# Logits of a row tile in one visit, and one PSUM bank for each block product of the walk

## The chip, the cores and the metric

The kernel runs on one NeuronCore of a Trainium2 chip. Its measure is the device time in microseconds (us), median of several runs. A profile of one more execution gives a record of every instruction. Engines in it: PE is TensorE's matmuls, PEld its weight loads, DVE VectorE, ACT ScalarE, POOL GpSimd, SP the engine that issues most DMAs. Lines (L1109) are lines of the kernel before, unless it is said that they are the changed kernel's.

## The reference

Two layers on 2708 nodes with 256 features, each with a residual and a layer norm. Layer 0 takes two steps. In each, a bilinear attention over all nodes keeps, in every row, the largest probabilities up to a sum of 0.9 (top-p); beside it, the features walk over the adjacency matrix R with its rows normalised:

```python
q = X @ W1.T @ W2.T;  k = X @ W3.T;  logits = q @ k.T          # 64 wide
A = softmax(logits), cut per row to the top 0.9, renormalised   # top-p
R = adj + I;  R = R / R.sum(-1)
for n in range(2):                                              # steps
    A = top_p_attention(Xa); Xf = R @ Xf; Xa = A @ Xa
    Z = Z + Xf @ U1[n].T + Xa @ U2[n].T
x = layernorm(x + layernorm(X + Z))
```

Layer 1 is a graph attention with four heads of 64, masked by the adjacency matrix, with a softmax over the first axis; `x = layernorm(x + that)`. Everything is in 32-bit floats.

## The kernel before

**Row tiles.** The nodes are cut into 22 row tiles (`NT`), 16 of 128 rows and 6 of 110. For each row tile and step the kernel makes the logits against all nodes, the exponentials `e` (a row of 2708), the top-p search, and then the attention product.

**Attention.** `step` (L1307) goes over the row tiles, and `weigh` (L274) over six groups of column tiles (four tiles in each, two in the last): `turned` (L261) transposes a group of `e` on PE into the one transpose bank (`tr`), ScalarE copies it (`eT`), and PE multiplies. The transposes of the next group stand before the products of this one. After each group `between` calls `slot` (L1292), so a row tile has six slots, 0 to 5; the first transposes of the next row tile stand between slot 4 and slot 5.

**Slots.** A slot first advances the searches under way (`going`), then begins a new one for the row tile three ahead (in slot 4), advances the other work (`doing`: projections, norms, `sources` for layer 1) and the preparation of adjacency blocks (`mixes`, in step 0), and then spends a number of matmuls on the walk (`stream`, from `walks`, L1034), one matmul for each call. In step 1 the numbers are `SPEND_1`, 68 in a row tile. Engines keep the order in which the code writes this down (a manual schedule): every engine is a queue in that order, and waits come from data and buffers.

**Logits and search.** `scores` (L780) makes the logits in three pieces, of 512, 512 and 330 columns in each half of the nodes. The two halves lie on 64 rows of PE each, and run beside each other into the two banks of an `lg` tile (`ps_lg`, two tiles, four banks). After two pieces it yields, so that the third piece follows in slot 5. In step 1 a search then takes twelve slots: `survey` makes four tallies on ScalarE, `bound` and `candidates`, `settle` (sorting, ties) and the masked row at L965 are VectorE's. L965 of one row tile is issued in slot 4, right before the first transposes that read it.

**The walk.** R @ Xf is done in blocks of two row tiles by a scheme of seven products (`PRODUCTS`) in place of eight, with 11 matmuls in each product; 11 row pairs and two steps make 154 products. Their operands are loaded three products ahead. Products are added up in four chains: X (1 and 2), Y (6 and 7), Z (5 and 3), W (4). A chain's second product goes on adding in the first one's bank. There are two banks for the walk (`walk0`, `walk1`), with the attention's bank as a third while it is free. When a product ends, ScalarE copies it (1, 2, 5) or VectorE adds it to an earlier one (6, 7, 4, 3: L1119 to L1129), and GpSimd makes one sum (L1135). When the walk of step 0 ends, `reblend` (L1173) remakes the operands for step 1. After the last products of step 1, `finish` (L1261) scales a row tile's walk on ScalarE (L1265), adds up, and hands over to `norms` and `sources`.

**PSUM.** Eight banks: four for logits, two for the walk, one for the attention, one for transposes. Small products (projections, `sources`) take a bank from `free_bank` (L650): a walk bank as long as the walk has not begun, an `lg` tile afterwards.

**Layer 1** (L1496) begins when layer 0's buffers are given back; its first VectorE row is `pt` at L1606.

Of the kernel before, what the change touches and what calls it, by code (L numbers as in the profile page):

```python
# [16 lines left out]
P = 128  # L17
# [19 lines left out]
SPEND_BETWEEN, SPEND_1 = 14, (12, 11, 11, 12, 11, 11)  # L37
# [8 lines left out]
def kernel(  # L46
# [505 lines left out]
    def fast_layer0(ep, adjp):  # L552
# [89 lines left out]
        p1, y1, y2 = (spare_u[:, k * HALF : (k + 1) * HALF] for k in range(3))  # L642
        u_rows = u_sb[:, 1].rearrange("p c s d -> p (c s) d")
        lines = [u_rows[:, k, :] for k in range(4)]
        lines += [spare_u[:, c : c + D] for c in (3 * HALF, 3 * HALF + D)]
# [134 lines left out]
        def scores(s, t):  # L780

            m = rows[t]
            cols = slice(off[t], off[t + 1])
            e = ep.tile([P, N], F32, name="e")
            halves = e.rearrange("p (h n) -> p h n", h=2)
            zp = small.tile([P, 3], F32, name="zp")
            for n, (c0, w) in enumerate(pieces):
                lg = ps_lg.tile([P, 2, CHUNK], F32, name="lg")
                for h in range(2):
                    part = slice(h * DA, (h + 1) * DA)  # L790
                    nc.tensor.matmul(  # L791
                        lg[:m, h, :w], qT[part, cols], kT[s][part, c0 : c0 + w],
                        start=True, stop=True,
                    )
                nc.scalar.activation(  # L795
                    halves[:m, :, c0 : c0 + w], lg[:m, :, :w], AF.Exp,
                    accum_out=zp[:m, n : n + 1],
                )
                if n == 1:
                    yield  # L800
            z = facts[s][0][:m, t : t + 1]
            nc.gpsimd.tensor_add(z, zp[:m, 0:1], zp[:m, 1:2])
            nc.gpsimd.tensor_add(z, z, zp[:m, 2:3])
            tau = new("tau", m)
            nc.gpsimd.tensor_scalar(tau, z, TOP_P, None, op0=ALU.mult)
            return e, z, tau

        def new(name, m):
            return small.tile([P, 1], F32, name=name)[:m]
# [191 lines left out]
        def blend(name, j0, j1, k):  # L1001
# [23 lines left out]
            1: ("D11", "B11", "X"), 2: ("A12", "B21", "X"), 6: ("S2", "T2", "Y"),  # L1025
            7: ("S3", "T3", "Y"), 5: ("S1", "T1", "Z"), 3: ("S4", "B22", "Z"), 4: ("D22", "T4", "W"),
# [7 lines left out]
        def walks():  # L1034
# [43 lines left out]
            last_bank = 1  # L1078
            for at, (s, i, n) in enumerate(queue):
                a, b = 2 * i, 2 * i + 1  # L1080
                m = rows[a]
                _, name, chain = PRODUCTS[n]
# [7 lines left out]
                if at % 7 == 0:  # L1090
                    use, over = {}, set()
                    xa, xb = (rowp.tile([P, D + 1], F32, name="xw", bufs=4) for _ in range(2))
                    if order_of(s, i) is THREE:
                        home = dict(zip("XYZW", ((7 * i + k) % 3 for k in (0, 1, 2, 6))))
                    else:
                        k = 1 if last_bank == 0 else 0
                        home = dict(X=k, Y=1 - k, Z=k, W=1 - k)
# [8 lines left out]
                last_bank = home[chain]  # L1106
                for j in range(PAIRS):
                    k = rows[2 * j]
                    nc.tensor.matmul(  # L1109
                        ac, blk[:k, j, :], MOVING[name](j, k, w),  # L1110
                        start=start and j == 0, stop=j == PAIRS - 1, skip_group_check=True,
                    )
                    if j == PAIRS - 1:
                        over.add(n)
                        left = ac[:, :HALF]
                        if n == 1:
                            nc.scalar.copy(p1[:m], left)
                        elif n == 6:
                            nc.vector.tensor_add(y1[:m], left, p1[:m])  # L1119
                        elif n == 7:  # L1120
                            nc.vector.tensor_add(y2[:m], left, p1[:m])
                        elif n == 2:
                            nc.scalar.copy(xa[:m, :w], ac)  # L1123
                        elif n == 5:
                            nc.scalar.copy(xb[:m, HALF : HALF + w], ac)
                        elif n == 4:
                            nc.vector.tensor_add(xb[:m, :HALF], left, y2[:m])
                        else:
                            nc.vector.tensor_add(xa[:m, HALF:D], left, y1[:m])  # L1129
# [4 lines left out]
                        if n in (5, 7) and {5, 7} <= over:  # L1134
                            nc.gpsimd.tensor_add(xb[:m, HALF:D], xb[:m, HALF:D], y2[:m])  # L1135
# [145 lines left out]
        going, doing, stored, owing = [], [], set(), set()  # L1281
        early, walked, blending, begun, rows_kept = [], [], [], [], []
# [24 lines left out]
        def step(s, cur, spend):  # L1307
            turned_first = None
            for t in range(NT):
# [11 lines left out]
                def between(n):  # L1321
# [18 lines left out]
                    slot(spend[n], (s, t + 3) if n == len(groups) - 2 else None)  # L1340
# [55 lines left out]
        with tc.manual_schedule(engines=engines):  # L1396
# [434 lines left out]
```

## Time and profile before

| | us |
|---|---|
| median of 3 runs (1533.94 to 1536.61) | 1533.94 |
| profiled execution | 1534.79 |
| its span, first to last instruction | 1532.7 |
| step 0, first transposes to the last attention rows, about | 72 to 443 |
| step 1, the same, about | 514 to 1189 |
| layer 1, from the first VectorE row to the end | 1184 to 1533 |

Busy times are unions of an engine's rows over the span. A busy PE is not PE at its peak: matmuls are pipelined and their ends are modelled, so distances from start to start are the better measure of what a row costs. A 32-bit matmul stands in the records as two rows, a transpose as one; a few records are missing. The granted clock was 0.995 of full speed over the span.

### The profile page before, as it was taken

The numbers are of one execution on the slowest core, as the hardware profiler recorded it, in microseconds if no ns is written. First come the engines' busy times: TensorE is split into PE (matmuls) and PEld (weight loads), VectorE is DVE, ScalarE is ACT, GpSimd is POOL, SyncE is SP. The second block draws the span as 40 slices with busy tenths as digits, with TensorE's granted clock in tenths as the row PEclk, the third lists the DMA queues.
The fourth block names the chain that finished last, engine by engine and source line by source line (L and its number), as shares of the span: only waits on it lengthen the run. The fifth ranks groups of instructions, "written<-read, shape, count | busy, mean of one in ns | idle before, by whom it ended". The sixth has DMA issues, their size and how long they took to land. (4 is left out here: it accounts for less than half of the span.)

```text
span 1532.7 us, 29967 instructions
## 1 busy us (share of the span) xinstructions
PE 1492.8 (97%) x10537; PEld 1064.6 (69%) x10537; DVE 1277.1 (83%) x3749; ACT 804.9 (53%) x1495; POOL 594.5 (39%) x959
## 2 busy tenths in 40 slices
PE   8999999999999999999999999999999999999996
PEld 4477777776778889988988888887898223433343
DVE  3699888999714978888889898989895998999996
ACT  3444444444326556655655666666653344456474
POOL 0046657566013323323454554544444310035143
PEclk9999999999999999999999999999999999999998
DMA  6288888878037755554564555555455355334331
GB/s 166 66 246 277 247 247 281 266 234 255 12 102 235 211 165 167 161 162 137 159 199 142 165 183 170 182 166 178 137 151 178 109 172 167 100 104 135 88 105 53
DMA packets 214488, 255.97 MB, mean 167 GB/s; under 512 B 42145, under 2 KB 180541, under 8 KB 214329
## 3 DMA queue, kind: packets, MB, share of 16 engines
q1 hardware_dynamic: 205622, 246.62, 53.7%
q10 hardware_dynamic: 8707, 7.35, 1.5%
q8 instruction: 85, 1.39, 0.4%
q14 instruction: 74, 0.61, 0.1%
HBM read 190.10 MB, written 62.44 MB: 165 GB/s over the span
## 5 line engine op out<-in xcount | busy, mean ns | idle before, releaser
L816 ACT ACTIVATE junk<-e,minus,rth 128x2708 bf16<-128x2708 f32 (+1 forms) x88 | 232.9, 2646 | 52.5 <-POOL rth L848 51.7
L271 ACT COPY eT<-tr 128x512 f32<-128x512 f32 (+5 forms) x264 | 141.5, 536 | 199.0 <-PE tr L266 196.5
L284 PE MATMUL att<-xm,eT 128*128 128x256 f32 (+3 forms) x968 | 230.8, 379 | 0.3 <-ACT xa L1325 0.3
L284 PE MATMUL att<-ba,eT 128*128 128x256 f32 (+3 forms) x968 | 230.9, 379 | 0.0
L1618 PE MATMUL acc<-pt,v 128*32 128x512 f32 (+3 forms) x2112 | 222.9, 543 | 2.1 <-DVE pt L1606 1.1
L1606 DVE SCALAR_TENSOR_TENSOR pt<-e,tj,blk 128x1024 f32<-128x1024 f32 (+3 forms) x176 | 186.6, 1125 | 8.3 <-ACT xw L1265 5.4
L284 PEld LDWEIGHTS att<-xm,eT 128*128 128x128 f32 (+3 forms) x968 | 169.6, 186 | 22.0 <-ACT xa L1325 0.7
L284 PEld LDWEIGHTS att<-ba,eT 128*128 128x128 f32 (+3 forms) x968 | 169.5, 186 | 22.0 <-ACT eT L271 0.8
L795 ACT ACTIVATE e<-lg 128x1024 f32<-128x1024 f32 (+1 forms) x132 | 121.0, 921 | 105.7 <-PE lg L791 102.2
L1109 PE MATMUL walk<-xe,blk 128*128 128x128 f32 (+3 forms) x1386 | 172.9, 275 | 1.2 <-ACT xw L1123 0.7
L1109 PEld LDWEIGHTS walk<-xe,blk 128*128 128x128 f32 (+1 forms) x1386 | 164.4, 187 | 11.4 <-issue 7.4
L1618 PEld LDWEIGHTS acc<-pt,v 128*32 128x32 f32 (+1 forms) x2112 | 73.4, 109 | 130.8 <-issue 76.2
L266 PE MATMUL tr<-ident,e 128*128 128x128 f32 (+3 forms) x968 | 147.5, 271 | 4.8 <-ACT eT L271 4.8
L266 PEld LDWEIGHTS tr<-ident,e 128*128 128x128 f32 (+3 forms) x968 | 111.3, 139 | 47.1 <-issue 26.7
L1109 PE MATMUL walk<-xm,blk 128*128 128x128 f32 (+3 forms) x1034 | 131.3, 277 | 5.4 <-DVE u_sb L1119 2.9
L1109 PEld LDWEIGHTS walk<-xm,blk 128*128 128x128 f32 (+3 forms) x1034 | 124.2, 188 | 14.0 <-issue 6.1
L1628 PE MATMUL acc<-pt,sb 128*32 128x512 f32 (+3 forms) x1056 | 115.7, 542 | 0.0
L1606 DVE SCALAR_TENSOR_TENSOR pt<-r,tj,blk 128x1024 f32<-128x1024 f32 (+1 forms) x88 | 109.9, 1312 | 1.3 <-issue 0.6
L247 ACT ACTIVATE blk<-blk 128x1024 f32<-128x1024 f32 (+3 forms) x66 | 63.3, 960 | 82.5 <-DMA blk<-in_adjT_dram 76.2
L896 DVE MAX8 cand<-e 128x8 f32<-128x170 f32 (+1 forms) x352 | 85.9, 320 | 21.1 <-ACT e L795 21.0
L896 DVE MAX8 cand<-scr 128x8 f32<-128x97 f32 (+1 forms) x616 | 102.8, 244 | 0.0
L914 DVE MAX8 top<-work 128x8 f32<-128x128 f32 (+3 forms) x242 | 82.3, 340 | 8.3
(283 smaller groups left out, 2410.2 us busy)
## 6 DMA issues: line engine op xcount, KB each, us to landing
blk<-in_adjT_dram SPq DMA_DIRECT2D x68, 512.0 KB
blk<-S SPq DMA_DIRECT2D x48, 512.0 KB
blk<-D SPq DMA_DIRECT2D x24, 512.0 KB
blk<-in_adjT_dram SPq DMA_DIRECT2D x26, 440.0 KB
D<-blk SPq DMA_DIRECT2D x16, 512.0 KB
S<-scr SPq DMA_DIRECT2D x16, 512.0 KB
S<-blk SPq DMA_DIRECT2D x16, 512.0 KB
xm<-S SPq DMA_DIRECT2D x16, 512.0 KB
```

Source lines behind the costliest of these rows:

```text
L247: nc.scalar.activation(bar, bar, AF.Sign)
L266: nc.tensor.transpose(tr[: rows[t], q, :m], e[:m, off[t] : off[t + 1]], ident[:m, :m])
L271: copy(eT[:k, : len(grp), :m], tr[:k, : len(grp), :m])
L284: nc.tensor.matmul(acc, eT[: rows[t], q, :m], value(t), start=(t == 0), stop=(t == NT - 1),)
L795: nc.scalar.activation(halves[:m, :, c0 : c0 + w], lg[:m, :, :w], AF.Exp, accum_out=zp[:m, n : n + 1],)
L816: nc.scalar.activation(junk[:m], e[:m], func, scale=rth, bias=minus1[:m], accum_out=acc)
L896: nc.vector.max(cand[:, n, :], src[:m, n * size : min(N, (n + 1) * size)])
L914: nc.vector.max(top[:, k : k + 8], work if k else flat)
L1109: nc.tensor.matmul(ac, blk[:k, j, :], MOVING[name](j, k, w), start=start and j == 0, stop=j == PAIRS - 1, skip_group_check=True,)
L1606: nc.vector.scalar_tensor_tensor(pt[:k, :gw], targets[g][h // 2][:k, h % 2, :gw], tj[:k, j, h : h + 1], bar, op0=ALU.max, op1=ALU.mult,)
L1618: nc.tensor.matmul(acc[h // 2][c][to : to + SIDE, :w], v[j][:k, h, o : o + SIDE], probs[n][h][:k, c0 : c0 + w], **at,)
L1628: nc.tensor.matmul(acc[2][c][h * SIDE : (h + 1) * SIDE, :w], sb[:k, j, h : h + 1].to_broadcast([k, SIDE]), probs[n][h][:k, c0 : c0 + w], **at,
```

## The change

1. **Logits.** In step 0 once the walk's preparation is under way (`begun`), and in all of step 1's row tiles that are begun inside `step` (`attending`), the third piece follows the first two in the same visit. It doesn't use an `lg` tile: its two halves go into `walk0` and `walk1`, and each half has an exponential of its own (four partial sums in `zp` in place of three, with one more small add on GpSimd). In step 1 all exponentials are issued in that visit; in step 0 those of the third piece are issued a slot later. In step 1 the new search is begun ahead of the others' advance.
2. **Slots.** In step 1 slot 4, the logits' slot, spends nothing on the walk, and slot 5 spends two products; for the last three row tiles, which begin no search, slot 4 spends one. A product that is open when logits are due is run to its end first.
3. **The walk's products.** Each has a bank of its own, the two walk banks in turn (three banks in turn in the order `THREE`, as before), and is taken out by itself: product 2 is now added to product 1 by VectorE in place of a copy on ScalarE, product 7 is added to `y1`, and GpSimd adds product 5 into `y1` before product 3 is added to that. `p1` is one column wider.

```diff
-SPEND_BETWEEN, SPEND_1 = 14, (12, 11, 11, 12, 11, 11)
+SPEND_BETWEEN = 14
+SPEND_1, SPEND_LAST = (11, 11, 11, 11, 0, 22), (11, 11, 11, 11, 11, 22)
...
-            zp = small.tile([P, 3], F32, name="zp")
+            zp = small.tile([P, 4], F32, name="zp")
+            one_visit = (begun and not walking) or attending
+            if attending:
+                while open_product:
+                    next(stream)
...
             for n, (c0, w) in enumerate(pieces):
+                if one_visit and n == 2:
+                    homes = [
+                        ps_wk.tile([P, CHUNK], F32, name=f"walk{h}")[:m, :w] for h in range(2)
+                    ]
+                    for h, home in enumerate(homes):
+                        logits(home, h, c0, w)
+                    if not attending:
+                        yield
+                    for h, home in enumerate(homes):
+                        nc.scalar.activation(
+                            halves[:m, h, c0 : c0 + w], home, AF.Exp,
+                            accum_out=zp[:m, n + h : n + h + 1],
+                        )
+                    if attending:
+                        yield
+                    continue
...
-                if n == 1:
+                if n == 1 and not one_visit:
                     yield
...
+            if one_visit:
+                nc.gpsimd.tensor_add(z, z, zp[:m, 3:4])
...
-                start = chain not in use
-                if start:
-                    pool, label = (ps_wk, f"walk{home[chain]}") if home[chain] < 2 else (ps_at, "att")
-                    use[chain] = pool.tile([P, CHUNK], F32, name=label)
+                home = at % 3 if order_of(s, i) is THREE else int(home == 0)
                 w = HALF + 1 if s == 0 and n in (1, 2, 5) else HALF
-                ac = use[chain][:m, :w]
+                pool, label = (ps_wk, f"walk{home}") if home < 2 else (ps_at, "att")
+                ac = pool.tile([P, CHUNK], F32, name=label)[:m, :w]
...
+                    open_product[:] = [at] if j < PAIRS - 1 else []
...
                         if n == 1:
-                            nc.scalar.copy(p1[:m], left)
+                            nc.scalar.copy(p1[:m, :w], ac)
+                        elif n == 2:
+                            nc.vector.tensor_add(xa[:m, :w], ac, p1[:m, :w])
                         elif n == 6:
-                            nc.vector.tensor_add(y1[:m], left, p1[:m])
+                            nc.vector.tensor_add(y1[:m], left, p1[:m, :HALF])
                         elif n == 7:
-                            nc.vector.tensor_add(y2[:m], left, p1[:m])
-                        elif n == 2:
-                            nc.scalar.copy(xa[:m, :w], ac)
+                            nc.vector.tensor_add(y2[:m], left, y1[:m])
...
                         if n in (5, 7) and {5, 7} <= over:
+                            nc.gpsimd.tensor_add(y1[:m], y1[:m], xb[:m, HALF:D])
                             nc.gpsimd.tensor_add(xb[:m, HALF:D], xb[:m, HALF:D], y2[:m])
...
         def slot(spend, begin=None):
 
-            advance(going)
-            if begin and begin[1] < NT:
-                going.append(search(*begin))
-                next(going[-1])
+            new = [search(*begin)] if begin and begin[1] < NT else []
+            if not attending:
+                advance(going)
+            for part in new:
+                next(part)
+            if attending:
+                advance(going)
+            going.extend(new)
...
-                    slot(spend[n], (s, t + 3) if n == len(groups) - 2 else None)
+                    turns = SPEND_LAST if s and t + 3 >= NT else spend
+                    slot(turns[n], (s, t + 3) if n == len(groups) - 2 else None)
...
+            attending.append(True)
             step(1, ba, SPEND_1)
```

More of the change, by code (lines that the diff above doesn't have):

```diff
@@ L641, in fast_layer0 @@
         spare_u = u_sb[:, 0].rearrange("p c s d -> p (c s d)")
-        p1, y1, y2 = (spare_u[:, k * HALF : (k + 1) * HALF] for k in range(3))
+        p1 = spare_u[:, 0 : HALF + 1]
+        y1, y2 = (spare_u[:, c : c + HALF] for c in (HALF + 1, D + 1))
         u_rows = u_sb[:, 1].rearrange("p c s d -> p (c s) d")
         lines = [u_rows[:, k, :] for k in range(4)]
-        lines += [spare_u[:, c : c + D] for c in (3 * HALF, 3 * HALF + D)]
+        lines += [spare_u[:, c : c + D] for c in (2 * D, 3 * D)]
         walking = []
@@ L785, in scores, with logits @@
             halves = e.rearrange("p (h n) -> p h n", h=2)
-            zp = small.tile([P, 3], F32, name="zp")
-            for n, (c0, w) in enumerate(pieces):
+            zp = small.tile([P, 4], F32, name="zp")
[3 more added lines that the diff above has]
+                    next(stream)
+            def logits(home, h, c0, w):
+                part = slice(h * DA, (h + 1) * DA)
+                nc.tensor.matmul(
+                    home, qT[part, cols], kT[s][part, c0 : c0 + w], start=True, stop=True
+                )
+            for n, (c0, w) in enumerate(pieces):
+                if one_visit and n == 2:
[10 more added lines that the diff above has]
+                            accum_out=zp[:m, n + h : n + h + 1],
+                        )
+                    if attending:
+                        yield
+                    continue
                 lg = ps_lg.tile([P, 2, CHUNK], F32, name="lg")
                 for h in range(2):
[L790 to L794, printed above, removed]
+                    logits(lg[:m, h, :w], h, c0, w)
                 nc.scalar.activation(
@@ L1024, in fast_layer0 @@
         PRODUCTS = {
-            1: ("D11", "B11", "X"), 2: ("A12", "B21", "X"), 6: ("S2", "T2", "Y"),
-            7: ("S3", "T3", "Y"), 5: ("S1", "T1", "Z"), 3: ("S4", "B22", "Z"), 4: ("D22", "T4", "W"),
+            1: ("D11", "B11"), 2: ("A12", "B21"), 6: ("S2", "T2"), 7: ("S3", "T3"),
+            5: ("S1", "T1"), 3: ("S4", "B22"), 4: ("D22", "T4"),
         }
@@ L1077, in walks @@
             yield
-            last_bank = 1
+            home = 1
             for at, (s, i, n) in enumerate(queue):
@@ L1081, in walks @@
                 m = rows[a]
-                _, name, chain = PRODUCTS[n]
+                _, name = PRODUCTS[n]
                 while s and (
@@ L1090, in walks @@
                 if at % 7 == 0:
-                    use, over = {}, set()
+                    over = set()
                     xa, xb = (rowp.tile([P, D + 1], F32, name="xw", bufs=4) for _ in range(2))
[L1093 to L1097, printed above, removed]
                 if at % 7 == (3 if s else 0):
                     aside = {t: beside(s, t) for t in (a, b)}
-                start = chain not in use
-                if start:
-                    pool, label = (ps_wk, f"walk{home[chain]}") if home[chain] < 2 else (ps_at, "att")
-                    use[chain] = pool.tile([P, CHUNK], F32, name=label)
+                home = at % 3 if order_of(s, i) is THREE else int(home == 0)
                 w = HALF + 1 if s == 0 and n in (1, 2, 5) else HALF
-                ac = use[chain][:m, :w]
-                last_bank = home[chain]
+                pool, label = (ps_wk, f"walk{home}") if home < 2 else (ps_at, "att")
+                ac = pool.tile([P, CHUNK], F32, name=label)[:m, :w]
                 for j in range(PAIRS):
                     k = rows[2 * j]
+                    open_product[:] = [at] if j < PAIRS - 1 else []
                     nc.tensor.matmul(
                         ac, blk[:k, j, :], MOVING[name](j, k, w),
-                        start=start and j == 0, stop=j == PAIRS - 1, skip_group_check=True,
+                        start=j == 0, stop=j == PAIRS - 1,
                     )
@@ L1281, in fast_layer0 @@
         going, doing, stored, owing = [], [], set(), set()
+        attending, open_product = [], []
         early, walked, blending, begun, rows_kept = [], [], [], [], []
```

## The prediction

> **What bounds the kernel now.** I read the page's busy rows first, then the table of stretches by row tile, then the timeline of one row tile of the second step, then the waits. The busy row and the slices of the page:
>
> ```profile
> PE 1492.8 (97%) x10537; PEld 1064.6 (69%) x10537; DVE 1277.1 (83%) x3749; ACT 804.9 (53%) x1495; POOL 594.5 (39%) x959
> ...
> PE   8999999999999999999999999999999999999996
> ...
> DVE  3699888999714978888889898989895998999996
> ```
>
> TensorE is never idle for long until the last slice, so a gain must come out of TensorE's own time; VectorE is the only other engine that is nearly full. By row tile (the columns are the stretch, its length, then busy us of PE, PEld, DVE, ACT, POOL), one tile of step 0, one early and one late tile of step 1, each from logits to logits:
>
> ```profile
> 101.93:119.61 17.68, 17.68 (x89) 13.02 (x88) 16.95 (x49) 8.04 (x18) 9.02 (x11) 1.00 0.95 268
> ...
> 626.99:657.15 30.16, 30.16 (x216) 26.77 (x215) 26.47 (x104) 18.14 (x24) 9.27 (x21) 1.00 0.53 164
> ...
> 941.36:973.71 32.35, 32.35 (x228) 28.55 (x227) 30.97 (x114) 21.64 (x43) 16.78 (x29) 1.00 0.55 167
> ```
>
> VectorE has 0.7, 3.7 and 1.4 us left in these: TensorE is the bound, and late in step 1 VectorE is close behind. Now the logits of one row tile, from the timeline (start, length, engine, line):
>
> ```profile
> 653.57 3.03 DVE L965 SCALAR_TENSOR_TENSOR e<-scr,fact,e 128x2708 f32<-128x2708 f32 x1
> ...
> 655.33 1.89 PE L284 MATMUL att<-ba,eT 110*128 110x256 f32 x8
> ...
> 657.15 1.99 PE L791 MATMUL lg<-kT,qT 64*128 64x512 f32 x8
> ...
> 658.33 1.02 ACT L795 ACTIVATE e<-lg 128x1024 f32<-128x1024 f32 x1 [2.43 <-PE lg L791]
> 659.07 0.71 PE L1109 MATMUL walk<-xe,xm 110*128 110x129 f32 x4
> ...
> 661.62 0.60 PE L266 MATMUL tr<-ident,e 128*128 128x128 f32 x4
> ...
> 663.02 0.83 PE L791 MATMUL lg<-kT,qT 64*128 64x330 f32 x4
> ...
> 663.78 0.71 PE L1109 MATMUL walk<-xm,blk 110*128 110x128 f32 x4
> ```
>
> The tile pays for two visits to 64-row matmuls. I take start-to-start times of the TensorE rows, since ends are modelled. In a run of attention rows the spacing is 0.216 us, but the last one before a visit takes 0.309: 0.093 to go in. Inside, a pair of 512 columns steps 0.430, the first pair 0.534: 0.104. The last pair takes 0.526 to the next row: 0.096 to come out. The third piece alone (663.02 to 663.78) takes 0.757 where two pairs of 330 columns at the same speed per column take 2 x 0.277 = 0.554, and 0.093 before it. So a visit costs **0.29 us** beyond its columns, and this repeats to 0.02 us in all visits.
>
> **The Trainium skill.** "TensorEngine Tiling (Array Packing)", Key Properties: a change of tiling mode drains TensorE. The trace agrees, with the 0.29 us. The same page, Restrictions and Gotchas (PSUM Pressure): different row tiles must write different PSUM banks. The change keeps this (one bank for each half), and the old two-bank logits tile did too. "PSUM — Partial Sum Buffer", PSUM bank collisions: writes and reads of one bank are to be ordered by semaphores, by bank. So in the new place the third piece waits for the last product's eviction, and a walk product for the exponentials; the trace of before has no such wait, so I place them by hand below.
>
> **The change part by part.**
>
> *One visit instead of two*, 19 row tiles in each step (the first three of either step keep two). Removed: 38 x 0.29 = 11.0 us of TensorE. In step 0 something comes back: there, the transposes two groups later reuse the one transpose bank, whose copy on ScalarE stands behind two exponentials. In the tile at 101.93 that copy ran to 105.74. After the change TensorE comes there at 101.93 + 2.48 (visit: 1.82 for two pieces + 0.66) + 0.44 (four transposes) + 0.86 (four attention rows) = 105.71, and needs about 0.1 with the semaphore: 19 x 0.1 = 1.9 us given back. Step 0: 5.5 - 1.9 = **-3.6**. In step 1 two walk products lie between, and the first of them wants the bank of the first half's exponential: it comes at visit + 3.78, and ScalarE is there at 1.18 + 2 x 1.01 + 0.45 = 3.65 (0.45 for 330 columns, from 1.02 for 1024 and 0.72 for 660). No wait, with 0.13 us to spare: step 1 **-5.5**.
>
> *Waits of layer-1 sources on the logits banks.* Four late row tiles have work of `sources` straight behind the first visit, in a logits buffer still to be read:
>
> ```profile
> PE lg L165 <- ACT e L795: 1.3, 3, 0.6
> ...
> PE lg L171 <- ACT e L795: 0.7, 2, 0.4
> ```
>
> Start to start these cost 4 x 0.43 + 0.73 = 2.4 us. After it, 0.66 us of third piece stand ahead, and the first exponential is done at visit + 2.2 against 2.48: **-2.4**.
>
> *A bank per product.* Same 154 x 11 matmuls. Product 2 now goes out as a VectorE add (0.28 us, row of L1129) instead of a ScalarE copy: 22 x 0.28 = 6.2 us on VectorE, 0.24 a tile; a GpSimd add of 0.86 us for each of 22 row pairs, and 38 small adds of 0.25. These lie beside TensorE; without that cover, the 6.2 us are the price. The third product's add now waits for GpSimd's; between lie two products and a transpose group, 7 us, and GpSimd is half idle. Zero in the sum.
>
> *No walk product in the logits' slot, two in the next.* The sum per tile goes from 68 to 66 walk matmuls. The order takes 11 walk matmuls (2.46 us) out of the place between the visit and the first transposes of the next row tile, which wait for the masked row, L965 on VectorE. In before these transposes start 1.8 to 6.4 us after L965's end, while that end stands from 3.8 us before to 2.2 us after the visit's start. Afterwards they want it at visit + 2.48. VectorE from the first slot's eviction to that end: sort 6.4, ties 3.1, replacing 3.85, mask 3.1, evictions 0.9 = 17.4 us; TensorE over the same way 3 x 4.65 + 4.5 = 18.45. One us of slack, which norms (0.8 and 0.4 us pieces, some waiting on GpSimd, once for 2.11 us) eat in some of the ten late tiles: **+2** (0 to 8). At the change of walk step, around 785 to 805, VectorE carries the blends of the operands (8.5 us from 784.7) besides; TensorE lost 3.7 us there, 2.7 of them for an eviction. The eviction gets more room now, the masked row less, about 5 us in all by the same counting: **+1**.
>
> *The end of the walk.* In before, the walk ends in slot 1 of the last row tile, and layer 1's first VectorE row waits for what ScalarE makes of its last product:
>
> ```profile
> 1177.28 0.60 PE L1109 MATMUL walk<-xe,blk 110*110 110x128 f32 x4
> ...
> 1177.92 0.29 DVE L1129 TENSOR_TENSOR xw<-walk,u_sb 110x128 f32<-110x128 f32 x1 [4.42 <-PE walk L1109]
> ...
> 1183.02 0.52 ACT L1265 ACTIVATE xw<-xw,rinv 110x256 f32<-110x256 f32 x1
> ...
> 1183.58 1.28 DVE L1606 SCALAR_TENSOR_TENSOR pt<-e,tj,blk 128x1024 f32<-128x1024 f32 x1 [5.37 <-ACT xw L1265]
> ```
>
> With 66 a tile, and 77 in the last three, it ends in slot 2: one group of four (0.44 + 1.73 us, less small work moved) no longer covers these 5.7 us: **+2** (0 to 2.6). Layer 1 itself is untouched.
>
> Sum: -3.6 - 5.5 - 2.4 + 2 + 1 + 2 = **-6.5 us**. Against the profiled execution (1534.79, span 1532.7 and 2.1 around it) that is 1528.3; against the median of the runs, 0.85 lower, 1527.4. I forecast 1527.4. About 0.2%, 3 us here, is what a measurement of this kernel can tell from no change.
>
> **Rivals.**
>
> A. Full gain: VectorE and the tail give nothing back, and the scattered stalls in the walk shrink with a steadier beat. -11.0 - 2.4 = -13.4: 1520.5. For it: VectorE's slack in early tiles (3.7 us a tile). Against: the step-0 copy and the shorter tail can be read off the order.
>
> B. Absorbed: VectorE at 30.97 of 32.35 us in a late tile plus 0.24 leaves 0.4 at the new period of about 31.6 (0.29 for the visit, 0.45 for two matmuls less). Then each of the ten late tiles comes out 0.5 us worse than in the likeliest case, which takes back more than what joining the visits gives it: -6.5 + 5 = -1.5: 1532.4, no change.
>
> C. Slower: the transposes of the next tile wait for the masked row in every tile of step 1. Without term +2 for that wait the sum is -8.5; over 19 tiles the gain is gone at 0.45 us a tile and slower by 0.2% from 0.61. At 0.9 us it is +8.6: 1542.5. For it: the closest tile in before (941.36, mask done at 943.56) would keep 0.28 us. Against: the mask is emitted in the same place in both orders, and the table shows VectorE with idle time in every tile.
>
> That the visits are not joined is no rival: the changed program's order has all six logits matmuls in a row in these 38 tiles.
>
> **How the numbers follow.** The likeliest 0.48, A 0.24, B 0.14, C 0.14. The likeliest's own range is 1523 to 1530.5: term by term, the wait for the mask between 0 and 4, the tail between 0 and 2.6, the change of walk step between -1 and +2. The range of 8 in 10 takes in A and B and the near side of C: 1519 to 1536. Faster by over 0.2% (under 1530.9): the likeliest nearly whole, A whole, a little of B: 0.74. Within 0.2%: most of B, the edges of the likeliest and of C: 0.14. Slower: 0.12.
>
> **What would show it.** Right: row tiles of step 0 at about 17.5 and 16.6 us for 17.7 and 16.8; of early step 1 at 29.4 to 29.5 for 30.16 (0.29, and 0.45 which is only moved to the last three tiles); the logits rows twelve in a row; no waits of L165 and L171 lines on exponentials; layer 1's first VectorE row about 4.5 us earlier than 1183.58. Wrong: a wait of the transposes on the mask of more than half a us in most tiles of step 1 (C), late tiles no shorter than in before (B), waits of walk matmuls on the exponentials, or a wait of the third piece on an eviction, which I put at nothing.

## The result, and the profile after

The changed kernel takes 1542.3 us (median of 8 runs, 1538.3 to 1543.7), the kernel before 1534.6 in the same runs: a ratio of 1.0044 on record, with an interval of 1.0035 to 1.0053 (the quotient of the two medians is 1.0050). It is slower by 0.4%, where 6.5 us, also 0.4%, faster was forecast. Its profiled execution has a span of 1537.6 us, 4.9 above that of before; it is the second fastest of the eight, so that the trace shows less than the whole loss of about 7 us.

The busy rows and slices of the changed kernel's page look like those of before; nothing in them shows the loss:

```profile
PE 1487.5 (97%) x10537; PEld 1070.3 (70%) x10537; DVE 1289.6 (84%) x3771; ACT 800.6 (52%) x1549; POOL 632.6 (41%) x1019
```

The table of stretches does, from one logits visit to a later one (length, then busy us of PE, PEld, DVE, ACT, POOL). The last three columns are the granted clock of TensorE, the share of the DMA engines and GB/s. In order: a row tile of step 0, an early and a late one of step 1, the two row tiles at the change of walk step, and the eight late ones together:

```profile
101.36:119.09 17.73, 17.70 (x90) 13.15 (x89) 17.01 (x49) 8.17 (x20) 9.63 (x12) 1.00 0.94 268
...
625.58:654.90 29.32, 29.32 (x211) 26.38 (x210) 25.96 (x99) 18.10 (x26) 10.65 (x23) 1.00 0.53 163
936.90:969.05 32.15, 30.64 (x218) 27.33 (x217) 30.05 (x114) 18.31 (x32) 17.87 (x35) 1.00 0.51 165
771.35:840.45 69.10, 62.12 (x421) 55.05 (x420) 60.97 (x211) 36.26 (x53) 38.80 (x61) 0.96 0.53 159
840.45:1097.36 256.91, 251.08 (x1765) 221.16 (x1764) 232.51 (x887) 164.65 (x332) 134.20 (x259) 1.00 0.53 164
```

The two row tiles at the change of walk step in the kernel before:

```profile
776.87:811.93 35.06, 31.98 (x215) 28.21 (x214) 30.92 (x106) 18.29 (x25) 19.91 (x27) 0.95 0.51 159
811.93:843.09 31.16, 30.44 (x216) 26.86 (x215) 28.27 (x109) 18.61 (x26) 15.64 (x32) 1.00 0.52 154
```

The early tile is 0.84 us shorter than before's 30.16, a tenth more than forecast. The tile of step 0 is not shorter (17.68 before). At the change of step TensorE stands idle for 7.0 us, where it was 3.8 before; in the eight late row tiles for 5.8 of 256.9 us, where it was 3.6 of 260.3.

The granted clock has a part in it. In the trace of before it falls to one half for 3.4 us from 801.5 us, in the changed kernel's twice, from 800.3 and from 837.8 us (both traces have a longer such stretch at the very end). From 60 to 1500 us the 19 traces of this case have 38 of these stretches, 3.4 or 6.8 us long, and each begins between 1.3 us before and 2.3 us after the end of a TensorE wait of 1.9 us or more; 23 such waits have none. So a wait of TensorE may cost more than its own length; no run tests this by itself. Over its eight executions the changed kernel's clock is 0.9935 on the mean, and 0.9954 to 0.9958 over those of the kernel before beside the experiments. Among the latter, 0.001 less of clock goes with 1.1 to 1.4 us more of time; an estimate from these figures is that 2 to 3 us of the loss go with the clock.

To set the stages against each other, the walk matmuls that the change moves to the end must come out: 36 of them leave the 18 row tiles from 536 to 1103 us, 8.05 us at 0.2235 each, and lie behind the last visit. With that done, the difference from before to after in the two profiled executions, in us:

| stage | forecast | measured |
|---|---|---|
| start, up to the first visit | 0 | -0.6 |
| step 0 | -3.6 | +0.9 |
| between the steps | 0 | +0.8 |
| step 1, eight early row tiles | -2.3 | -3.0 |
| two row tiles at the change of walk step | +0.4 | +3.8 |
| eight late row tiles | -4.7, and most of the +2 for the mask | +0.2 |
| behind the last visit | +2, and one visit's -0.3 | +2.8 |
| sum | -6.5 | +4.9 |

So the gain of step 1's early visits came and step 0's did not, and something at the change of step and in the late row tiles took the rest: of the 11.4 us between forecast and measured, step 0 has 4.5, the change of step 3.4 and the late row tiles 2.9.

**Step 0.** The timeline around the second visit of before (start, length, engine, line; in brackets the idle time and who ended it):

```profile
105.30 0.82 PE L791 MATMUL lg<-junk,qT 64*128 64x330 f32 x4
...
105.63 0.50 ACT L1325 ACTIVATE xa<-att,rden 128x256 f32<-128x256 f32 x1
...
106.55 1.03 PE L284 MATMUL att<-xm,eT 128*128 128x256 f32 x4
```

and the same place in the changed kernel:

```profile
104.59 0.58 ACT L272 COPY eT<-tr 128x512 f32<-128x512 f32 x1
...
105.23 0.42 PEld L267 LDWEIGHTS tr<-ident,e 128*128 128x128 f32 x4 [0.28 <-ACT eT L272]
...
105.39 0.47 ACT L1351 ACTIVATE xa<-att,rden 128x256 f32<-128x256 f32 x1 [0.22 <-PE att L285]
...
105.92 1.16 PEld L285 LDWEIGHTS att<-xm,eT 128*128 128x128 f32 x6 [0.27 <-ACT xa L1351]
```

There is one bank for the attention. The copy `xa` empties it at the end of a row tile, and the next row tile's first attention row must wait for it. In before, the third piece's visit stood between the two and hid the copy. Without it TensorE waits: the transposes lose 0.09 us (forecast as 0.1), and the attention rows begin at 105.92, where 105.23 + 0.44 for four transposes would have been 105.67: 0.25 more. 0.09 + 0.25 - 0.29 = +0.05 us a row tile, 19 times +0.9.

**Late in step 1.** In the view of waits (who waited for whom: us in total, times, longest) the kernel before has

```profile
PE tr L266 <- ACT eT L271: 4.8, 5, 1.3
ACT junk L816 <- POOL rth L848: 51.7, 22, 6.0
POOL ln_rs L139 <- DVE ln_ve L137: 45.1, 16, 5.0
```

and the changed kernel

```profile
PE tr L267 <- ACT eT L272: 7.5, 6, 2.6
ACT junk L843 <- POOL rth L875: 63.8, 22, 9.2
POOL ln_rs L140 <- DVE ln_ve L138: 53.6, 20, 5.0
```

The longest of the first row, on ScalarE, GpSimd and TensorE, in order of time:

```profile
827.94 0.55 POOL L140 TENSOR_TENSOR ln_rs<-ln_ve,minus_half 128x1 f32<-128x1 f32 x1 [3.76 <-DVE need L961]
828.46 0.73 POOL L1291 TENSOR_TENSOR u_sb<-ca,cb 128x256 f32<-128x256 f32 x1
...
833.62 0.19 POOL L875 TENSOR_TENSOR rth<-rth,g 128x1 f32<-128x1 f32 x1
833.84 2.64 ACT L843 ACTIVATE junk<-e,minus,rth 128x2708 bf16<-128x2708 f32 x1 [7.54 <-POOL rth L875]
836.49 0.56 ACT L272 COPY eT<-tr 110x512 f32<-110x512 f32 x1
837.10 0.43 PE L267 MATMUL tr<-ident,e 128*110 128x128 f32 x2 [2.62 <-ACT eT L272]
```

To be read backwards. The transposes wait for ScalarE's copy of the group before. The copy stands behind a tally (L843), the tally waits for its threshold (`rth`) from GpSimd, and GpSimd came to it late, because it had stood 3.76 us at a norm's power (L140), waiting for a sum that VectorE made behind the sort (the row names `need`, which ended last; the sum, `ln_ve`, was made at 827.71). The Trainium skill, "PSUM — Partial Sum Buffer", Engine vs sequencer instructions, says that ScalarE, VectorE and GpSimd work off their queues strictly first in, first out; this chain is that, three times over.

### The profile page after: what moved, and what is told of

Same layout as the page of the kernel before. It is cut to its first block, busy times and chain, and to the rows that moved or that the text cites. A ratio compares the mean times of both kernels' runs of the same rounds, so it can differ in the third digit from the quotient of the medians.

```text
span 1537.6 us, 30151 instructions
## 1 busy us (share of the span) xinstructions
PE 1487.5 (97%) x10537; PEld 1070.3 (70%) x10537; DVE 1289.6 (84%) x3771; ACT 800.6 (52%) x1549; POOL 632.6 (41%) x1019
## 5 line engine op out<-in xcount | busy, mean ns | idle before, releaser
L843 ACT ACTIVATE junk<-e,minus,rth 128x2708 bf16<-128x2708 f32 (+1 forms) x88 | 232.9, 2646 | 64.6 <-POOL rth L875 63.8
L1129 PE MATMUL walk<-xe,blk 128*128 128x128 f32 (+3 forms) x1386 | 166.2, 276 | 4.7 <-POOL rth L875 3.3
L267 PEld LDWEIGHTS tr<-ident,e 128*128 128x128 f32 (+3 forms) x968 | 110.6, 139 | 49.4 <-ACT e L820 17.4
L820 ACT ACTIVATE e<-lg 128x1024 f32<-128x1024 f32 (+2 forms) x94 | 93.6, 1001 | 94.6 <-PE lg L796 89.4
L1129 PE MATMUL walk<-xm,blk 128*128 128x128 f32 (+3 forms) x1034 | 123.6, 275 | 3.8 <-DVE none L981 1.7
L1129 PEld LDWEIGHTS walk<-xm,blk 128*128 128x128 f32 (+3 forms) x1034 | 120.5, 187 | 7.0 <-DVE few L977 1.8
```

Of the source, the lines that this page charges most:

```text
L267: nc.tensor.transpose(tr[: rows[t], q, :m], e[:m, off[t] : off[t + 1]], ident[:m, :m])
L820: nc.scalar.activation(halves[:m, :, c0 : c0 + w], lg[:m, :, :w], AF.Exp, accum_out=zp[:m, n : n + 1],)
L843: nc.scalar.activation(junk[:m], e[:m], func, scale=rth, bias=minus1[:m], accum_out=acc)
L1129: nc.tensor.matmul(ac, blk[:k, j, :], MOVING[name](j, k, w), start=j == 0, stop=j == PAIRS - 1,)
```

## The experiments

Each ratio is to the kernel before, run beside it; one thousandth is 1.5 us.

### Step 0: two visits again, or the visit moved

Two visits in step 0, all else as changed:

```diff
-            one_visit = (begun and not walking) or attending
+            one_visit = bool(attending)
```

> The changed kernel with step 0's logits back in two visits; step 1 and the walk stay changed. If joining the visits in step 0 gains nothing (my reading of the traces: the third piece alone used to cover ScalarE's copy of the attention bank, and without it TensorE waits for that copy in each of 19 row tiles), the time stays where the changed kernel is: 1.0044 times the kernel before, give or take 0.0005, about 1541.3. If the forecast's 3.6 us are there after all, it is slower by them: 1.0068, about 1545.

Measured: 1.0032 (1.0021 to 1.0043). So step 0's 3.6 us are not there; if anything two visits are better. Then one slot later, so that the joined visit stands behind a row tile's last attention rows:

```diff
-                    slot(turns[n], (s, t + 3) if n == len(groups) - 2 else None)
+                    slot(turns[n], (s, t + 3) if n == len(groups) - 1 - s else None)
```

> The changed kernel with step 0's search begun one slot later, so that the joined visit stands behind the last attention rows of a row tile and covers the copy of the attention bank. If that copy is what took step 0's gain: 0.2 to 0.29 us in each of 19 row tiles, 4 to 5.5 us faster than the changed kernel, 1.001 to 1.002 times the kernel before, row tiles of step 0 at about 16.6 and 17.45 us. If something else (ScalarE as a whole, VectorE, the clock) took it: no gain, 1.0044, row tiles at 16.85 and 17.7.

Measured: 1.0026 (1.0016 to 1.0036), 2.8 us (give or take 2) faster than the changed kernel, where 4 to 5.5 were expected. Up to 320 us its row tiles alternate between about 17.4 and 16.5 us, 0.33 shorter than in the changed kernel. Further on a new loss comes in: at 324 and 344 us transposes wait 1.0 and 3.4 us for the masked row, and from 343 us the clock is half for 6.8 us. In this trace, of the slowest of 22 executions, these take back what the visits gave. Its timeline ahead of that:

```profile
102.48 1.99 PE L796 MATMUL lg<-junk,qT 64*128 64x512 f32 x8
102.59 0.47 ACT L1351 ACTIVATE xa<-att,rden 128x256 f32<-128x256 f32 x1 [0.23 <-DVE fact L949]
...
104.96 0.66 PE L267 MATMUL tr<-ident,e 128*128 128x128 f32 x4
...
105.45 1.89 PE L285 MATMUL att<-xm,eT 128*128 128x256 f32 x8
```

The copy (102.59 to 103.06) lies under the visit, and the attention rows follow the transposes without a wait. The same edit alone on the kernel before, with the changed kernel's lines for the third piece's two banks in step 0:

```diff
+            one_visit = begun and not walking
...
-                    slot(spend[n], (s, t + 3) if n == len(groups) - 2 else None)
+                    slot(spend[n], (s, t + 3) if n == len(groups) - 1 - s else None)
```

> The kernel before with one edit: in step 0 the logits of a row tile are made in one visit, begun in slot 5, so that it covers ScalarE's copy of the attention bank and of the transposes. Step 1 and the walk are those of before. If the joined visit is worth 0.27 us in each of 19 row tiles as soon as it covers the copy: 5 us faster than the kernel before, 0.9967. If ScalarE's exponentials, or the copies behind them, take it back: 1.000.

Measured: 0.9977 (0.9969 to 0.9986). Start to start, 17 row tiles are 5.0 us shorter; the whole of step 0 gains 3.8, as the first of these visits comes later. The waits for the masked row don't come there. So in step 0 the joined visit is worth its 0.29 us in a row tile where it covers the copy and the mask is in time.

### Which engine empties product 2's bank

```diff
-                            nc.vector.tensor_add(xa[:m, :w], ac, p1[:m, :w])
+                            nc.scalar.copy(xa[:m, :w], ac)
+                            nc.vector.tensor_add(xa[:m, :w], xa[:m, :w], p1[:m, :w])
```

> The changed kernel with product 2's bank freed by a ScalarE copy, as in the kernel before, and the addition of product 1 done by VectorE afterwards, from SBUF. If the later row tiles lose because a bank now waits for VectorE's queue (waits of 1.4 to 3.5 us at 796, 883 and 1108 us): about 4 to 6 us faster than the changed kernel, 1.001 to 1.002. If the two products in one slot or GpSimd's additions do it: same as the changed kernel within 1.5 us, 1.0035 to 1.005.

Measured: 1.0081 (1.0064 to 1.0097). Neither: slower still by 5.7 us. The waits of walk matmuls on VectorE at 883 and 1108 us went, but the transposes' on ScalarE's copy grew from 7.5 to 11.8 us and those on the masked row from 1.2 to 4.8; and the trace has four stretches of half clock, where the changed kernel's has two. My reading that VectorE's eviction is the culprit fell.

### The walk alone

The changed walk (bank for each product, new additions) in the slots and visits of before:

```diff
-SPEND_1, SPEND_LAST = (11, 11, 11, 11, 0, 22), (11, 11, 11, 11, 11, 22)
+SPEND_1 = (12, 11, 11, 12, 11, 11)
...
-            one_visit = (begun and not walking) or attending
...
-            attending.append(True)
```

> The kernel before with the changed walk alone: a bank for each product, products 2 and 7 added by VectorE and one more sum on GpSimd; visits and slots are those of before. The forecast priced this at nothing: 1.000. If the evictions are what makes the later row tiles lose: 3 to 6 us slower than the kernel before, 1.002 to 1.004. If the order of the slots (none beside the logits, two in the next) does it: 1.000 within 0.0005.

Measured: 1.0003 (0.9994 to 1.0012). In its trace the late row tiles are 2.2 us longer, the change of step 2.0 shorter, most of which is that its clock never falls there. The products' banks, VectorE's additions and GpSimd's are worth nothing in sum in the slots and visits of before; so the loss lies with the slots and the visits, or with what the banks do together with them.

### Step 1: visits and slots

The second product of slot 5 moved to slot 1, then one product in every slot, slot 4's ahead of the logits:

```diff
-SPEND_1, SPEND_LAST = (11, 11, 11, 11, 0, 22), (11, 11, 11, 11, 11, 22)
+SPEND_1, SPEND_LAST = (11, 22, 11, 11, 0, 11), (11, 22, 11, 11, 11, 11)
```

```diff
-SPEND_1, SPEND_LAST = (11, 11, 11, 11, 0, 22), (11, 11, 11, 11, 11, 22)
+SPEND_1, SPEND_LAST = (11, 11, 11, 11, 11, 11), (11, 11, 11, 11, 11, 22)
...
             new = [search(*begin)] if begin and begin[1] < NT else []
+            if attending and new:
+                for _ in range(spend):
+                    if next(stream, True):
+                        break
+                spend = 0
```

> The changed kernel with the two products of slot 5 shared out as one in slot 5 and two in slot 1; the logits' slot stays without one, the sum per row tile stays 66. In the changed kernel's late row tiles the transposes wait for ScalarE's copy, which stands behind a tally that waits for GpSimd's and VectorE's chain (2.8, 1.7, 0.9 and 1.3 us at 834, 965, 999 and 1063 us). If the order of the slots does that, an earlier product covers it, and the walk ends a slot earlier: 4 to 8 us faster than the changed kernel, 0.999 to 1.002 times the kernel before. If it is VectorE's total load there: no gain, 1.003 to 1.005, and the same time lost at other rows.

> The changed kernel with one walk product in every slot of step 1, in slot 4 ahead of the logits visit. The transposes of the next row tile stand as close behind the visit as in the changed kernel, but VectorE has the 2.4 us of a product more before the masked row; on the other hand the first product after the visit wants a bank whose exponential ends 0.3 to 0.8 us after TensorE comes there, and the third piece wants a bank that VectorE has just to empty. If two products in one slot are what makes the changed kernel lose: 2 to 6 us faster than it, 1.0005 to 1.003. If the banks' waits come in every row tile: 5 to 15 us slower, 1.008 to 1.014.

Measured: 1.0071 (1.0058 to 1.0084) and 1.0244 (1.0228 to 1.0260). With two products in slot 1 the waits behind late tallies are gone, as thought, but in most row tiles the product of slot 5 waits 0.2 us for the exponential in its bank (the early ones are 0.42 us longer for it), and late waits turn up elsewhere (2.5 us of a walk matmul up to 999 us, 1.5 of `sources` up to 969). The other is rival C in the flesh. Its waits:

```profile
PE tr L267 <- ACT eT L272: 17.0, 12, 3.9
PE tr L267 <- DVE e L992: 12.4, 12, 1.4
```

VectorE takes out slot 4's product, which ends just as the visit begins, and only then makes the masked row (629.88 and 630.09 us, visit at 629.70). The 3.03 us of the mask are longer than the 2.48 of the visit, so the next transposes wait 1.0 to 1.4 us. These waits are 12.4 of the 31 us that this run is slower than the changed kernel; those for the copy grew from 7.5 to 17.0. That slot 4 is empty in the changed kernel is what keeps this from happening there.

Two visits again in step 1, with the slots as changed: first with products that run across slots, then with an open product run to its end ahead of the logits, as in the changed kernel.

```diff
-            one_visit = (begun and not walking) or attending
-            if attending:
-                while open_product:
-                    next(stream)
+            one_visit = begun and not walking
...
```

```diff
-            one_visit = (begun and not walking) or attending
+            one_visit = begun and not walking
             if attending:
                 while open_product:
                     next(stream)
...
```

> The changed kernel with step 1's logits in two visits again, third piece in slot 5 in a logits tile; the slots (none in the logits' slot, two products in slot 5) and the walk stay changed. If joining the visits gives 0.29 us in every row tile of step 1 and saves the sources their waits: 5.5 to 8 us slower than the changed kernel, 1.008 to 1.010. If the late row tiles are bound by VectorE: only the eight early ones show it, early row tiles at 29.6 us for 29.3, 2 to 3 us slower in all, 1.005 to 1.0065.

> The changed kernel with step 1's logits in two visits again (the third piece in slot 5, in a logits tile, ahead of the two products), and with an open product still run to its end ahead of the logits, so that every product begins and ends where it does in the changed kernel. If the joined visit is worth 0.29 us in a row tile: early row tiles at 29.6 us for 29.3, and 2.5 to 5.5 us slower than the changed kernel, 1.006 to 1.008 times the kernel before. If the 33 us that the other run with two visits lost came from the two visits and not from products cut by the slots: 1.02 or more. The transposes behind the visit come 0.66 us earlier here: if the masked row is as close as the changed kernel's 0.7 and 0.8 us at two places say, they wait for it more often.

Measured: 1.0262 (1.0244 to 1.0279) for the first, which keeps no product whole and so didn't tell the two apart: TensorE waits 9.7 and 8.6 us for evictions of walk products. The second: 1.0101 (1.0087 to 1.0115), early row tiles at 29.67 us for 29.32, and 4.3 us of waits for the mask. So the joined visit in step 1 is worth 8.7 us (give or take 2.6) in these slots, about 3 of them because the waits for the mask are fewer. It is a gain; by difference, the slots lose more. With two visits the late waits of the transposes for ScalarE's copy are there as well (2.6, 0.7, 0.8 and 1.1 us): it is not the joined visit that brings them.

### The end of the walk

11 matmuls more in slot 1 of the last three row tiles, so that the walk ends earlier (by 6.5 us in the trace); then, in place of that, 11 more in five late row tiles; then the second of these with step 0's visit in slot 5.

```diff
-SPEND_1, SPEND_LAST = (11, 11, 11, 11, 0, 22), (11, 11, 11, 11, 11, 22)
+SPEND_1, SPEND_LAST = (11, 11, 11, 11, 0, 22), (11, 22, 11, 11, 11, 22)
```

```diff
                     turns = SPEND_LAST if s and t + 3 >= NT else spend
+                    if s and t in (10, 12, 14, 16, 18):
+                        turns = (11, 22, 11, 11, 0, 22)
```

> The changed kernel with 11 more walk matmuls in each of the last three row tiles (in slot 1), so that the walk ends two or three slots earlier. If the end of the walk behind the last attention rows is what costs 2 to 3 us at the start of layer 1: 2 to 3 us faster than the changed kernel, 1.0025 to 1.003. If VectorE's and GpSimd's other work of the last row tiles sets that start: the same as the changed kernel, 1.0044 within 0.0007.

> The changed kernel with one more walk product (11 matmuls, 2.4 us of TensorE) in slot 1 of five late row tiles (10, 12, 14, 16 and 18), so that as much is missing from the last row tiles, where VectorE has few searches left. If the late row tiles are bound by VectorE, so that walk taken out of them doesn't shorten them and lengthens the end, then walk put back into them is partly free: 4 to 8 us faster than the changed kernel, 0.999 to 1.002 times the kernel before. If TensorE bounds the late row tiles as it does the early ones, the work is only moved: what the earlier end of the walk is worth, as with more walk in the last three row tiles, 1.001 to 1.002, and the five row tiles each 2.4 us longer.

> The changed kernel with both repairs: step 0's joined visit in slot 5, and one more product in five late row tiles. If the two losses are separate, they add up: 8 to 13 us faster than the changed kernel, 0.996 to 0.999 times the kernel before. If one hides the other: no better than the better one alone, 1.0005 to 1.002.

Measured: 1.0013 (1.0005 to 1.0021), 0.9979 (0.9972 to 0.9986) and 0.9963 (0.9948 to 0.9979); the first two are faster than either reading had them. In the first two traces the way from the last visit to the end is 435.3 and 423.4 us, 440.2 in the changed kernel: 4.9 us for the earlier end alone, and 11.9 more for the five products that left. The eight late row tiles, which took four of the five, grew by 9.7 us, as much as four products cost (2.46 us each); so TensorE bounds them as it does the early ones, and my reading of a VectorE bound there fell. The fifth went to the two row tiles at the change of step, and these became 1.2 us shorter: with it, the transposes' wait of 2.6 us at 837 us is gone, and the second stretch of half clock too. And the kernel before, with step 0's visit in slot 5 and 11 more in three row tiles:

```diff
+                    turns = spend
+                    if s and t in (14, 16, 18):
+                        turns = (12, 22, 11, 12, 11, 11)
```

> The kernel before with step 0's joined visit in slot 5, and 11 more walk matmuls in slot 1 of the row tiles 14, 16 and 18 of step 1. If VectorE bounds the late row tiles in the kernel before too: 2 to 5 us faster than with the joined visit alone, 0.9945 to 0.997. If TensorE bounds them there: nothing but an earlier end of the walk, which ends early enough already, 0.9975 to 0.999.

Measured: 0.9932 (0.9919 to 0.9944), 6.9 us better than with the visit alone, which is more than either reading had expected, and the lowest ratio of all. Behind the last visit the trace is 12.3 us shorter than with the visit alone, where the three products that left are 7.4: 4.9 us for the earlier end, as in the changed kernel. The walk ends too late in both kernels: the layer that follows waits for it.

### GpSimd behind VectorE

The power of a norm a slot later, when VectorE's sum has long been made, in the changed kernel and in that of before (each norm ends a slot later; a row tile has two, so the "four" in the first expectation should be two):

```diff
         rs = small.tile([P, 1], F32, name="ln_rs")
+        yield
         nc.gpsimd.tensor_tensor(rs[:m], ve[:m], minus_half[:m], op=ALU.pow)
```

> The changed kernel with GpSimd's power of a norm issued one slot later than VectorE's sum that it needs, so that GpSimd doesn't stand waiting for VectorE with the chain to the next tally behind it. If that wait (3.8 and 4.0 us of GpSimd before the late tallies at 833.8 and 963.5 us) is what makes ScalarE's copy of the transposes late: the four waits of 2.8, 1.7, 0.9 and 1.3 us go away, 3 to 6 us faster than the changed kernel, 1.0005 to 1.0025. If the tallies are late for another reason (GpSimd's own work, VectorE's sums late as well): same as the changed kernel, 1.0035 to 1.005. The norms end four slots later, which lies beside the attention.

> The kernel before with the one edit that made the changed kernel 10 us faster: GpSimd's power of a norm issued one slot later. If GpSimd standing behind VectorE is a loss that the change brought (its order of slots): the kernel before gains little, 0.998 to 1.000, for its waits of transposes on ScalarE's copy sum to 2 us less in step 1. If both kernels carry it alike, so that it says nothing of the change: 0.993 to 0.995, as much as in the changed kernel.

Measured: 0.9977 (0.9967 to 0.9987), 10.2 us (give or take 2) faster than the changed kernel, more than the 3 to 6 expected, and 0.9963 (0.9950 to 0.9976) for the kernel before with it, 5.7 us faster than without and between the two readings. The changed kernel's waits with the edit:

```profile
ACT junk L844 <- POOL rth L876: 52.6, 22, 9.3
...
POOL ln_rs L141 <- DVE ln_ve L138: 8.8, 4, 4.6
...
PE tr L268 <- ACT eT L273: 2.7, 3, 1.1
```

and the tally and copy that came at 833.84 and 836.49:

```profile
829.48 2.65 ACT L844 ACTIVATE junk<-e,minus,rth 128x2708 bf16<-128x2708 f32 x1 [3.15 <-POOL rth L876]
...
832.12 0.56 ACT L273 COPY eT<-tr 110x512 f32<-110x512 f32 x1
```

The traces help to part what both kernels carry from what the change brought. From 771 to 1097 us, the two tiles at the change of step and the eight late ones, the changed kernel gains 5.7 us by the edit, the kernel before nothing (+0.6). Behind the last visit they gain 5.3 and 4.9; there, layer 1's first VectorE row waits 0.6 and 1.4 us, where it had waited 2.7 and 5.4. Part of the difference from 771 to 1097 us is the clock: with the edit, the changed kernel has 3.4 us of half clock there for 6.8, the kernel before 6.8 for 3.4. TensorE's idle time there falls from 12.8 to 9.6 us in the changed kernel and from 7.4 to 6.6 in before. In the runs, the two gains differ by 4.5 us, give or take 2.8. So this chain is a part of the change's loss, between about 2.5 and 6 us of it. In before it was there too, but it held up TensorE less.

Last, all three repairs on both kernels:

> The changed kernel with three repairs: step 0's joined visit in slot 5, one more product in five late row tiles, and the power of a norm a slot later. If the losses are separate: 0.9963 for the first two and 8 to 10 us less for the third, 0.990 to 0.992 times the kernel before. If the extra products already cover the late tallies, so that the second and the third repair do the same: 0.994 to 0.9963.

> The kernel before with the same three repairs (extra products in three late row tiles). If joining the visits in step 1 is worth what the early row tiles show, and its losses are repaired, this one is slower than the changed kernel with its repairs by 3 to 8 us: 0.992 to 0.994 times the kernel before. If the change is a loss in step 1 whatever is repaired: it is the faster one, 0.990 or less.

Measured: 0.9942 (0.9927 to 0.9957) and 0.9941 (0.9928 to 0.9954). They can't be told apart, nor from the 0.9932 above: the repairs overlap, and with them made, step 1 of the change is neither a gain nor a loss, to within 3 us.

## Why the prediction was wrong

- **Step 0 (-3.6): wrong, measured +0.9.** The step that failed is "in step 0 something comes back": it followed what the transposes' bank would wait for, and stopped there. The removed visit also covered `xa`, the copy of the one attention bank. With 0.25 us of that besides the 0.09 (forecast as 0.1), nothing of the 0.29 is left; under the copy, it is all there.
- **Step 1's visits (-5.5): right**, and rather low. The early row tiles took 29.32 us for the 29.4 to 29.5 forecast, and the visits undone cost 8.7 us in all, the sources' waits and more waits for the mask among them.
- **The sources' waits (-2.4): mostly right.** The five waits on the exponentials, 2.0 us in the view of waits, went; two of `sources` on their own copy, of 0.3 us each, came.
- **A bank for each product (0): right**, 1.0003.
- **The masked row (+2): near in size, not in place.** Two waits, 1.2 us in the view of waits, one at the change of step and one behind the last visit; none in the eight late row tiles. The 12 waits with a product in slot 4 show how close it is.
- **The change of step (+1): mis-sized.** The two row tiles with their visits were +0.4 and came out at +3.8. Both kernels lose about 3 us there to a product that waits for an eviction (2.7 us up to 802 before, 3.3 up to 800 after, where VectorE's row L1139 empties the bank), so the "more room" for it didn't come. On top come the late tally, 2.6 us of the transposes' time up to 837.10, and the second stretch of half clock right behind it. Where the tally's wait is gone (the power of a norm a slot later), there is one such stretch and the two row tiles take 65.1 us for the 69.1.
- **Late row tiles (-2.7 with their part of the mask, measured +0.2): a term was missing.** The step that failed is that VectorE's lateness was priced at the masked row alone, with "the table shows VectorE with idle time in every tile" against anything worse. I noted that VectorE sometimes waits for GpSimd, and did not look for the opposite: GpSimd waiting for VectorE, with the threshold of the next tally behind it, and ScalarE's copy behind that. It was in before's view of waits, `ln_rs` on `ln_ve` with 45.1 us, next to 4.8 us of TensorE's waits for the copy. After the change TensorE waited longer for it; putting the power a slot later took back 10.2 us in all. That emptying slot 4 and filling slot 5 moved TensorE's work away from the places that covered it fits the run with the second product in slot 1, where these waits are gone, but no run shows it alone.
- **The end (+2, 0 to 2.6): right in place, low in size**, +2.8 in the trace with a visit's 0.3 already taken off; layer 1's first VectorE row came at 1188.98 us, 5.4 later, where 4.5 earlier was forecast. That the walk's end costs some 5 us in the kernel before as well, I did not see.

Rival C named almost the time, 1542.5, by luck: of the loss the mask is 1.2 us. What stays open: which edit moves the tallies' cover (none in slot 4, two in slot 5, or the new search begun ahead of the others' advance, which stands in every run with the changed slots), how much of the loss is the clock's, and the 0.8 us between the steps, which no run took apart.

## What to carry to other kernels

When an edit takes TensorE work out of a place, list every copy that ran under it, for every bank, not just for the one that is next in line: the cover can be worth as much as the work, as in step 0. Watch the clock in the same table: the two runs in which TensorE waited longest (one product in every slot, and products cut by the slots) were granted least of it, 0.991 and 0.989 on the mean. Follow chains through the queues of helper engines to their end: an engine half idle can still be the late link, when a 0.2 us instruction stands behind one that waits for a third engine. And work that ends on the path to the next stage should be spent early; a few products moved ahead gave 5 to 10 us here, about as much as joining the visits.

## What the runs showed that I had not expected

One `yield` ahead of an instruction of 0.55 us was worth 10 us in one kernel and 6 in the other. A ScalarE copy in place of a VectorE addition to free a bank, with as many VectorE additions as without, cost 5.7 us, though ScalarE is busy for 52% of the span and VectorE for 84%. It was paid at the transposes, which waited longer for ScalarE's copy and for VectorE's masked row; tallies of 2.64 us stand in ScalarE's queue, but how much of it is theirs was not tested.
